# Layer 0's experts in a four-layer kernel: 64 own slots per expert instead of 128, two experts in one tile

## The chip, the cores and the metric

The kernel runs as one program on one core of a Trainium2 chip. A core has a matrix engine (TensorE; PE in the profile, PEld for the loading of its stationary operand), VectorE (DVE), ScalarE (ACT), GpSimd (POOL) and SyncE (SP). These work side by side and wait for each other through semaphores. 16 DMA engines move data between the device memory and the on-chip memory SBUF; matrix results land in the small on-chip memory PSUM. Transfers are put into queues by SP, by ACT and by POOL. All data is fp32.

The metric is the device time of one execution in microseconds (us). Before the change it is 2267.27 us, the median of three runs (2261.71 to 2273.08).

## What is computed

Tokens x of shape 2 x 512 x 256 (1024 tokens of width 256) go through four layers. Each adds a cross-attention to a context of 2 x 1024 x 256 and then a feed-forward part with eight experts. The change touches the feed-forward part of layer 0, in which each token goes to exactly one expert:

```python
def _L0_ffn_ref(hidden_states, router_w, router_b, w1, w2):
    x = hidden_states.reshape(-1, d)
    logits = x @ router_w + router_b
    route = softmax(logits, axis=1)
    max_prob = max(route, axis=1, keepdims=True)
    max_ind = argmax(route, axis=1)
    for e in range(num_experts):                 # 8
        h = x @ w1[e]                            # 256 -> 2 x 1024
        a, g = split(h, 2, axis=1)
        y = silu(a) * g @ w2[e]                  # 1024 -> 256
        out = where((max_ind == e)[:, None], y, out)
    return out * max_prob
...
x = x + _L0_ffn_ref(_layernorm(x, axis=-1), ...)
```

With the reference's inputs the router of layer 0 gives the eight experts 64, 19, 173, 147, 49, 28, 411 and 133 of the 1024 tokens.

## The kernel before

The kernel is written out in the order of the stages; a scheduling layer inserts the semaphore waits, and the order of instructions on each engine and of transfers in each queue is the order of the program, as the scheduler has laid it out. Names like `xs` or `w` are tiles; a pool gives each tag a fixed number of buffers (`bufs`), and a tile waits for the release of the buffer that it takes.

**Routing.** After layer 0's attention, `normed` gives the normalized tokens `xn`, `to_T` transposes them on TensorE into `xT`, and `router_logits` (L132, tile `pl`) forms the logits. `slots_of` (L332) ranks the tokens of each expert by a matmul with a triangular matrix (`pr`, L347 and L349) and gives each token a slot. An expert has 128 own slots, so slot tile e (128 rows of the array `xd`) belongs to expert e. What an expert has beyond 128 goes to overflow tiles of 128 rows, which are handed out in order of the experts. `wrow` holds, for each overflow tile, the rows of the weight array of its expert; `used` is the number of overflow tiles in use, read into a register. The thresholds, base numbers and triangular tables come as columns of one constant array, `c_route`.

**The tokens move.** `moe` scatters `xn` into `xd` by eight indirect transfers on POOL (L424, one for each 128 tokens). Then it calls a *filler* that gives TensorE something to do while this goes on: `first_batch` transposes the normalized context into `cT` and computes half of layer 1's keys and values in 16 jobs (`pk`, L555 and L575: a matmul group, a copy on ACT into one of two buffers, and a store to `kd` or `vd` through ACT's queue). The other half comes after the experts (`ahead1(..., 1)`).

**The slot tiles.** `slot_tile(s)` loads the weights of its expert, 128 partitions of 6144 numbers (3.1 MB), into `w`: the eight own tiles on SP's queue (L438), the overflow tiles by an indirect transfer on POOL's (L445). There are three `w` buffers. It reads its 128 rows of tokens (`xs`, L452), transposes them (`pt`, L460), copies them to `sT` (L462), and computes gate and up halves `pa` and `pg` (L132). Here 128 columns of weights are the stationary operand and the 128 tokens the moving one, so that the hidden activations come out transposed, as the next product needs them. ACT applies silu (L476), DVE multiplies (L477) into `hT`, the down product goes to `y` (L480), ACT copies it to `yo` (L507) and stores it to `yd`. Layer 0 always runs 8 own tiles and 6 overflow tiles (`ALWAYS`), in this order; a branch on `used > 6` (L501) runs a seventh. At the end `combine` gathers the rows of `yd` back to the tokens' order by eight indirect transfers on POOL (`yg`), multiplies by the gate and adds to X. Layers 1 to 3 use the same functions with their own sizes.

**What is next.** The attention of layer 1 reads `kd` and `vd` back: SP loads `kT` at L1021, and its first scores are at L1036.

Of the kernel before, what the change touches and what calls it, by code (L numbers as in the profile page):

```python
# [19 lines left out]
B = 2  # L20
# [13 lines left out]
def tile_kernel(ctx: ExitStack, tc: tile.TileContext, d: dict, out: bass.AP):  # L34
# [213 lines left out]
    def rt(name, shape=(TT, E)):  # L248
        return small.tile([P, *shape], F32, tag=f"rt_{name}", name=name, bufs=1)
# [81 lines left out]

    def slots_of(ps, picks, n_over):  # L332

        oh = rt("oh_all", (2 * TT + 1, E))
        nc.vector.memset(oh, 0.0)
# [8 lines left out]
        for k in range(1, TT + 1):  # L348
            nc.tensor.matmul(pr, ones, oh[:, TT - k : 2 * TT + 1 - k, :], start=False, stop=(k == TT))  # L349
        r = rt("rank_in", (TT + 1, E))  # L350
        nc.vector.tensor_copy(r, pr)
        more = rt("more", (E, 7))
        nc.vector.tensor_tensor(more, r[:, TT, :, None].to_broadcast([P, E, 7]), c_thr, ALU.is_gt)
        ov = rt("ov", (E,))
# [9 lines left out]
        nc.vector.scalar_tensor_tensor(  # L364
            sl, r[:, 0:TT, :], 128.0, base[:, None, :].to_broadcast([P, TT, E]), ALU.is_ge, ALU.mult
        )
# [35 lines left out]
    ALWAYS = {"L0": 6, "L1": 4, "L2": 11, "L3": 13}  # L402

    def moe(L, ps, hp, ep, rows, slots, wrow, used, F, act, glu, finish, filler=None, hold=None):

# [3 lines left out]

        n_over = wrow.shape[1]  # L410
        NS = E + n_over
        FT, W1 = F // P, (2 * F if glu else F)
# [21 lines left out]

        def slot_tile(s):
            w = ep.tile([P, WC], F32, tag="w", name="w")
            if s < E:
                x = nc.sync.dma_start(w, wd[s * P : (s + 1) * P, :]).ins  # L438
                if hold is not None and s < 4:
                    tc.add_manual_dep(  # L440
                        x, hold.name, mybir.DependencyInfo(mybir.DependencyClass.Sync, mybir.DependencyReason.DATA),
                        reason="not among the transfers that the attention waits for",
                    )
            else:
                nc.gpsimd.indirect_dma_start(  # L445
                    out=w, out_offset=None, in_=wd,
                    in_offset=bass.IndirectOffsetOnAxis(ap=wrow[:, s - E : s - E + 1], axis=0),
                )
            w1 = w[:, 0 : 2 * W1].rearrange("p (c f) -> p c f", c=2)
            w2 = w[:, 2 * W1 : 2 * W1 + FT * D].rearrange("p (t f) -> p t f", t=FT)  # L450
            xs = hp.tile([P, RW], F32, tag="xs", name="xs", bufs=4)
# [9 lines left out]
            sT = hp.tile([P, 2, P], F32, tag="sT", name="sT", bufs=3)  # L461
            nc.vector.tensor_copy(sT, pt)  # L462
            hT = hp.tile([P, FT, P], F32, tag="hT", name="hT")
            for f4 in range(0, FT, 4):
# [32 lines left out]

        always = E + ALWAYS[L]
        for s in range(always):
            slot_tile(s)  # L500
        with tc.If(used > ALWAYS[L]):  # L501
# [27 lines left out]

    def combine(hp, yd, slots, gates, dst):  # L530

        for t in range(TT):
            for i, si in enumerate(slots):
                yg = hp.tile([P, D], F32, tag="yg", name="yg", bufs=8)
                nc.gpsimd.indirect_dma_start(
                    out=yg, out_offset=None, in_=yd, in_offset=bass.IndirectOffsetOnAxis(ap=si[:, t : t + 1], axis=0)
                )
                to = dst[:, t, :]
                if gates is None:
                    nc.vector.tensor_add(to, to, yg)  # L540
                else:
                    nc.vector.scalar_tensor_tensor(to, yg, gates[i][:, t : t + 1], to, ALU.mult, ALU.add)
# [22 lines left out]
    def ahead1(ps, st, w, cT, b):  # L565

        if b == 0:
            kds["L1"] = dram.tile([B * 4 * P, S], F32, tag="L1kd", name="kd")
            vds["L1"] = dram.tile([B * S, 512], F32, tag="L1vd", name="vd")

        def values(pv, kt):
            r = slice(b * S + kt * P, b * S + (kt + 1) * P)
            mm2(pv, cT, r, w, slice(512, 1024))
            v = st.tile([P, 512], F32, tag="sv", name="sv", bufs=2)
            nc.scalar.copy(v, pv)  # L575
            nc.scalar.dma_start(vds["L1"][r, :], v)

        jobs = []
        for pr in range(4):
            for hf in range(2):  # L580
                jobs.append(("k", (b * 4 + pr) * P, hf * 512, slice(pr * P, (pr + 1) * P), b * S + hf * 512))
        jobs += [("v", kt) for kt in range(8)]
        ahead(ps, st, "L1", w, cT, jobs, values)
# [60 lines left out]
    def fill_slots():  # L644
# [6 lines left out]
        for L, NS, RW in (("L0", 15, D), ("L1", 15, D), ("L2", 23, D + 1), ("L3", 23, D + 1)):  # L651
            rows = NS * P + (2 * NT if RW > D else 0)
            xds[L] = [
                dram.tile([NS * P, RW], F32, tag=f"{L}xd", name="xd"), dram.tile([rows, D], F32, tag=f"{L}yd", name="yd")
            ]

            for to in xds[L][:1] if RW > D else (xds[L][0], xds[L][1][(E + ALWAYS[L]) * P :, :]):
                todo += [to[r : min(r + 4 * P, to.shape[0]), :] for r in range(0, to.shape[0], 4 * P)]
# [23 lines left out]
    with (  # L682
# [28 lines left out]
        route = load(const, [P, d["c_route"].shape[1]], d["c_route"], "route")  # L711
        c_thr = route[:, 0:56].rearrange("p (e j) -> p e j", e=E)
        c_tri = route[:, 56:120].rearrange("p (e f) -> p e f", e=E)
        c_iota = route[:, 120:240].rearrange("p (s e) -> p s e", e=E)
        c_base, c_first, c_part = route[:, 240:248], route[:, 248:256], route[:, 256:257]
        c_tok = route[:, 257:265]

# [223 lines left out]
    with (  # L941
        tc.tile_pool(name="L0f", bufs=1, reuse_waits="tile") as fp,
        tc.tile_pool(name="L0h", bufs=2, reuse_waits="tile") as hp,
        tc.tile_pool(name="L0g", bufs=3, reuse_waits="tile") as ep,
        psum(2, "L0fps") as ps,
    ):
        rw = load_rows(fp, d["L0_ffn_router_w"], "rw")
        rb = load_bc(fp, d["L0_ffn_router_b"], "rb")
        xT = fp.tile([P, 2, NT], F32, tag="xT", name="xT")
        xn = normed(fp, False)  # L950
# [9 lines left out]
        oh = first_of(lg, mp, "oh1")  # L960
        slots, wrow, used = slots_of(ps, [oh], 7)
        cT = fp.tile([P, 2, B * S], F32, tag="cT", name="cT")
# [6 lines left out]
        ahead1(ps, hp, wkv, cT, 1)  # L969
        combine(hp, yd, slots, [mp], X)  # L970

# [484 lines left out]
    with (  # L1456
# [28 lines left out]
        ahead16(ps, fp, "L2", params, 4)  # L1485
        combine(hp, yd, slots, None, X)

# [152 lines left out]
def _route():  # L1640


    e = np.arange(E, dtype=np.float32)
    row = np.concatenate([
        np.tile(128.0 * np.arange(1, 8), E),
        (e[None, :] < e[:, None]).ravel(),
        np.repeat(np.arange(15), E),
        128.0 * (E - 1 - e),
        128.0 * e,
    ]).astype(np.float32)  # L1650
    p = np.arange(P, dtype=np.float32)[:, None]
    return np.concatenate([np.tile(row, (P, 1)), p, p + 128.0 * np.arange(TT, dtype=np.float32)], axis=1)

# [105 lines left out]
```

## Time and profile before

| | us |
|---|---|
| median of three runs | 2267.27 |
| the profiled execution, its own time | 2271.06 |
| its span in the profile | 2269.0 |
| PE busy in it | 2087.4 |
| layer 0's slot tiles, first transpose to last product | 507.6 to 666.3 |
| the filler ahead of them | 471 to 508 |
| first scores of layer 1's attention | 706.98 |

The profile is one execution. Engines are busy side by side, so their busy times don't add up to the span. A row of the timeline gives start, duration, engine, line, operation, result and operands, shape and number of instructions; in brackets stands the idle time of the engine ahead of it and what ended it. A matmul in fp32 is recorded as several instructions: one logical matmul here is two records. The granted clock (PEclk) is the share of full speed at which TensorE may run; its mean over the execution is 0.962. DMA share is the mean share of time in which the 16 DMA engines are busy.

The weight transfers of layer 0's experts stand in the trace as follows:

| load | queue | issued at, us |
|---|---|---|
| own tiles 0 to 2 | SP | 459.75, 461.11, 469.9 |
| own tiles 3 to 7 | SP | 522.67, 533.3, 544.9, 555.5, 567.11 |
| overflow tiles 0 to 5 | POOL | 578.62, 589.58, 600.17, 611.79, 622.39, 634.01 |

The eight scatters into `xd` are at 492.52 to 502.6 on POOL, the reads `xs` begin at 504.62 on SP.

### The profile page before, as it was taken

The numbers are of one execution on the slowest core, as the hardware profiler recorded it, in microseconds if no ns is written. First come the engines' busy times: TensorE is split into PE (matmuls) and PEld (weight loads), VectorE is DVE, ScalarE is ACT, GpSimd is POOL, SyncE is SP. The second block draws the span as 40 slices with busy tenths as digits, with TensorE's granted clock in tenths as the row PEclk, the third lists the DMA queues.
The fourth block names the chain that finished last, engine by engine and source line by source line (L and its number), as shares of the span: only waits on it lengthen the run. The fifth ranks groups of instructions, "written<-read, shape, count | busy, mean of one in ns | idle before, by whom it ended". The sixth has DMA issues, their size and how long they took to land. (4 is left out here: it accounts for less than half of the span.)

```text
span 2269.0 us, 30730 instructions
## 1 busy us (share of the span) xinstructions
PE 2087.4 (92%) x11892; PEld 1267.6 (56%) x11892; DVE 1085.2 (48%) x2161; ACT 866.2 (38%) x1657; POOL 438.6 (19%) x420
## 2 busy tenths in 40 slices
PE   7999999999998999999898898899599999579996
PEld 3444444358984444555586344599333333479995
DVE  7766666741115656655313884110387773322223
ACT  4444444421115655555112333222135556223333
POOL 2222223210012111111101122312123310111110
PEclk9999999999999999999899999999789999689998
DMA  4222221277744101001454512687311101657771
GB/s 128 70 61 75 75 72 50 83 269 283 302 162 136 38 28 38 28 10 51 156 211 153 213 35 90 219 320 293 101 47 30 34 15 25 250 187 288 315 306 63
DMA packets 112328, 301.21 MB, mean 133 GB/s; under 512 B 23344, under 2 KB 76849, under 8 KB 103473
## 3 DMA queue, kind: packets, MB, share of 16 engines
q1 hardware_dynamic: 76624, 159.79, 21.0%
q0 software_dynamic: 9888, 104.49, 12.0%
q10 hardware_dynamic: 25664, 34.90, 4.3%
q8 instruction: 98, 1.61, 0.3%
q14 instruction: 54, 0.43, 0.1%
HBM read 243.42 MB, written 47.66 MB: 128 GB/s over the span
## 5 line engine op out<-in xcount | busy, mean ns | idle before, releaser
L1356 ACT ACTIVATE p<-s 128x512 f32<-128x512 f32 (+3 forms) x384 | 186.3, 546 | 176.2 <-PE s L1355 115.4
L132 PE MATMUL pa<-sT,w 128*128 128x128 f32 x1920 | 236.0, 277 | 10.7 <-DVE sT L462 3.7
L132 PEld LDWEIGHTS pa<-sT,w 128*128 128x128 f32 x1920 | 227.3, 193 | 19.3 <-ACT sq L1537 5.7
L480 PE MATMUL y<-w,hT 128*128 128x256 f32 x960 | 221.8, 383 | 12.4 <-DVE hT L477 6.3
L1298 PE MATMUL s<-kT,qT 32*128 32x512 f32 (+3 forms) x768 | 218.2, 613 | 10.0 <-DVE nm L1304 4.9
L480 PEld LDWEIGHTS y<-w,hT 128*128 128x128 f32 x960 | 178.5, 191 | 37.7 <-DVE hT L477 8.5
L1355 PE MATMUL s<-qA,kT 32*128 32x512 f32 (+3 forms) x768 | 196.1, 586 | 1.3 <-ACT p L1356 0.9
L1308 DVE TENSOR_REDUCE mx<-s 128x1 f32<-128x512 f32 x256 | 163.5, 686 | 56.1 <-PE s L1298 35.4
L477 DVE TENSOR_TENSOR hT<-act,pg 128x512 f32<-128x512 f32 x82 | 56.0, 688 | 233.5 <-PE pg L132 204.6
L1043 ACT ACTIVATE p<-s,nm 128x512 f32<-128x512 f32 x192 | 129.6, 687 | 84.0 <-DVE nm L1040 84.0
L132 PE MATMUL pg<-sT,w 128*128 128x128 f32 x1312 | 160.0, 275 | 1.3 <-ACT sv L575 1.3
L878 ACT ACTIVATE p<-s 128x1024 f32<-128x1024 f32 x128 | 124.3, 1023 | 89.7 <-PE s L873 89.7
L879 DVE TENSOR_SCALAR p<-p 128x1024 f32<-128x1024 f32 x128 | 108.9, 859 | 95.2 <-ACT p L878 95.2
L132 PEld LDWEIGHTS pg<-sT,w 128*128 128x128 f32 x1312 | 153.1, 192 | 1.4 <-ACT sv L575 1.4
L1040 DVE TENSOR_REDUCE nm<-s 128x2 f32<-128x1024 f32 x96 | 113.3, 1221 | 83.5 <-PE s L1036 83.5
L149 POOL TENSOR_TENSOR kT<-kT,turned 128x512 f32<-128x512 f32 x62 | 100.8, 1631 | 215.2 <-DVE turned L147 208.4
L884 DVE TENSOR_TENSOR acc<-acc,p 128x1024 f32<-128x1024 f32 x96 | 131.6, 1371 | 2.8
L804 PE MATMUL o<-p,v 128*64 128x512 f32 x512 | 125.7, 609 | 3.6 <-DVE p L879 3.6
L873 PE MATMUL s<-qT,kT 64*128 64x512 f32 x512 | 127.2, 615 | 0.0
L1298 PEld LDWEIGHTS s<-kT,qT 32*128 32x128 f32 x768 | 77.1, 191 | 66.7 <-issue 28.0
L1057 PEld LDWEIGHTS pt<-ident,p 128*128 128x128 f32 x768 | 86.3, 141 | 49.2 <-issue 24.5
L1331 PE MATMUL o<-p,v 128*32 128x256 f32 (+3 forms) x1280 | 106.2, 403 | 6.7 <-POOL p L1360 6.4
(282 smaller groups left out, 2955.3 us busy)
## 6 DMA issues: line engine op xcount, KB each, us to landing
w<-in_L_experts_dram SPq DMA_DIRECT2D x8, 3200.0 KB
w<-in_L_experts_dram SPq DMA_DIRECT2D x8, 3072.0 KB
w<-in_L_experts_dram SPq DMA_DIRECT2D x8, 2048.0 KB
w<-in_L_experts_dram SPq DMA_DIRECT2D x8, 1536.0 KB
kd<-sk ACTq DMA_DIRECT2D x40, 256.0 KB
kT<-kd SPq DMA_DIRECT2D x16, 512.0 KB
turned<-kT SPq DMA_DIRECT2D x60, 128.0 KB
v<-vd SPq DMA_DIRECT2D x12, 512.0 KB
```

What stands on the lines that cost most here:

```text
L132: nc.tensor.matmul(ps_ap, lhsT[:, dc, lcols], rhs[:, dc, rcols], start=(dc == 0), stop=(dc == 1))
L480: nc.tensor.matmul(y, hT[:, f, :], w2[:, f, :], start=(f == 0), stop=(f == FT - 1))
L804: nc.tensor.matmul(G[n]["o"][64 * j : 64 * j + 64, :], V[g, b][:, kt, pr * P + 64 * j : pr * P + 64 * j + 64], p[:, j, :], start=(kt == 0) ...
L873: nc.tensor.matmul(s1[:, j, :], G[n]["kT"][r, kt * P : (kt + 1) * P], G[n]["qT"][r, :], start=True, stop=True)
L878: G[n]["exp"] = nc.scalar.activation(p, s1, AF.Exp, scale=0.125).ins
L884: nc.vector.tensor_add(G[n]["acc"], G[n]["acc"], p)
L1040: nc.vector.tensor_reduce(nm[:, qt, :, c], s1, AX.X, ALU.max, negate=True)
L1043: nc.scalar.activation(p[:, j, :], s1[:, j, :], AF.Exp, bias=nm[:, qt, j, c : c + 1], accum_out=l[:, qt, j, c : c + 1],)
L1298: nc.tensor.matmul(s1[:, :w], qT[r, qt * P : (qt + 1) * P], kT[r, c * 512 : c * 512 + w], start=True, stop=True)
L1308: nc.vector.tensor_reduce(mx[:, qt, j, c : c + 1], s1, AX.X, ALU.max)
L1355: nc.tensor.matmul(s2[:, qs], kT[r, kt * P : (kt + 1) * P], qA[r, qs], start=True, stop=True)
L1356: nc.scalar.activation(p[:, j, qs], s2[:, qs], AF.Exp, scale=0.25)
```

## The change

In layer 0 each expert has 64 own slots. Two experts, 2s and 2s + 1, share *pair tile* s: its first 64 rows are slots of the one, the last 64 of the other. What an expert has beyond 64 tokens goes to overflow tiles of 128 rows, up to 11 of them. With the counts above 6 overflow tiles are in use, as before.

A pair tile loads both experts' weights on SP's queue. For gate and up the tokens are now the stationary operand, 64 columns at a time, and 512 columns of weights move. Tokens of the first expert write PSUM partitions 0 to 63, those of the second 64 to 127, in alternating matmuls. The hidden activations then stand with tokens on partitions, and are transposed on TensorE (`turn`) ahead of the down product, which works in the same two halves.

Order: pair 0, overflow 0, pair 1, overflow 1, pair 2, overflow 2, pair 3, overflow 3, overflow 4, overflow 5; the branch on `used > 6` holds five more. `FRONT` is the number of tiles of own slots.

Further edits: four `w` buffers in layer 0; its transposed tokens `xT` and `cT` share a buffer (tag "cT"); the values `sv` of the filler share the two buffers of `sk`; `combine` writes its gathers into one tile for all tokens (layer 0: in the buffer of `xn`) instead of eight rotating ones, for layers 0 and 1; the constant array is 80 columns wider. `yd`'s zero fill starts behind the ten tiles.

```diff
-    def slots_of(ps, picks, n_over):
+    def slots_of(ps, picks, n_over, first_of_expert=P):
+        c_thr, c_base, c_first = firsts[first_of_expert]
...
-        more = rt("more", (E, 7))
-        nc.vector.tensor_tensor(more, r[:, TT, :, None].to_broadcast([P, E, 7]), c_thr, ALU.is_gt)
+        nj = c_thr.shape[2]
+        more = rt(f"more{nj}", (E, nj))
+        nc.vector.tensor_tensor(more, r[:, TT, :, None].to_broadcast([P, E, nj]), c_thr, ALU.is_gt)
...
+    FRONT = {"L0": E // 2, "L1": E, "L2": E, "L3": E}
...
+        def pair_tile(s):
+            ws = []
+            for j in range(2):
+                w = ep.tile([P, WC], F32, tag="w", name="w")
+                nc.sync.dma_start(w, wd[(2 * s + j) * P : (2 * s + j + 1) * P, :])
+                ws.append(parts(w))
+            sT = turned_slots(s)[1]
+            hT = hp.tile([P, FT, P], F32, tag="hT", name="hT")
+            y = ps.tile([P, D], F32, tag="y", name="y")
+            hs = {}
+            def half(tag, c0):
+                pa = ps.tile([P, 512], F32, tag=tag, name="p" + tag)
+                for dc in range(2):
+                    for j in range(2):
+                        cols = slice(64 * j, 64 * j + 64)
+                        nc.tensor.matmul(
+                            pa[cols, :], sT[:, dc, cols], ws[j][0][:, dc, c0 : c0 + 512], start=(dc == 0), stop=(dc == 1)
+                        )
+                return pa
+            def hidden(c, pa, pg):
+                a = hp.tile([P, 512], F32, tag="act", name="act")
+                nc.scalar.activation(a, pa, act)
+                nc.vector.tensor_mul(a, a, pg)
+                hs[c] = a
+            def turn(c):
+                pt = ps.tile([P, 4, P], F32, tag="mm", name="pt")
+                for f in range(4):
+                    nc.tensor.transpose(pt[:, f, :], hs[c][:, f * P : (f + 1) * P], ident)
+                nc.vector.tensor_copy(hT[:, 4 * c : 4 * c + 4, :], pt)
+            def product(c):
+                for f in range(4 * c, 4 * c + 4):
+                    for j in range(2):
+                        cols = slice(64 * j, 64 * j + 64)
+                        nc.tensor.matmul(
+                            y[cols, :], hT[:, f, cols], ws[j][1][:, f, :], start=(f == 0), stop=(f == FT - 1)
+                        )
+            pa = half("a", 0)
+            hidden(0, pa, half("g", F))
+            pa = half("a", 512)
+            turn(0)
+            hidden(1, pa, half("g", F + 512))
+            product(0)
+            turn(1)
+            product(1)
...
-        for s in range(always):
-            slot_tile(s)
+        if front == E:
+            for s in range(always):
+                slot_tile(s)
+        else:
+            for s in range(front):
+                pair_tile(s)
+                slot_tile(front + s)
+            for s in range(2 * front, always):
+                slot_tile(s)
...
-                yg = hp.tile([P, D], F32, tag="yg", name="yg", bufs=8)
+                yg = rows[:, t, :]
...
-            v = st.tile([P, 512], F32, tag="sv", name="sv", bufs=2)
+            v = st.tile([P, 512], F32, tag="sk", name="sv", bufs=2)
...
-        tc.tile_pool(name="L0g", bufs=3, reuse_waits="tile") as ep,
+        tc.tile_pool(name="L0g", bufs=4, reuse_waits="tile") as ep,
...
-        xT = fp.tile([P, 2, NT], F32, tag="xT", name="xT")
+        xT = fp.tile([P, 2, B * S], F32, tag="cT", name="xT")
...
-        slots, wrow, used = slots_of(ps, [oh], 7)
+        slots, wrow, used = slots_of(ps, [oh], 11, 64)
```

## The prediction

> **What bounds the kernel now.** I read the busy totals first, then the stage that the change touches in windows, then single instructions in it.
>
> ```profile
> PE 2087.4 (92%) x11892; PEld 1267.6 (56%) x11892; DVE 1085.2 (48%) x2161; ACT 866.2 (38%) x1657; POOL 438.6 (19%) x420
> ```
>
> ```profile
> 475.00:480.00 5.00, 5.00 (x36) 3.92 (x35) 1.07 (x2) 1.82 (x4) 0.00 (x0) 1.00 1.01 429
> 507.60:666.30 158.70, 153.95 (x1150) 145.66 (x1148) 24.47 (x42) 23.54 (x44) 5.69 (x6) 1.00 0.67 257
> 710.00:715.00 5.00, 3.87 (x12) 1.55 (x13) 2.35 (x3) 3.65 (x12) 0.71 (x1) 0.71 1.12 264
> ```
>
> The columns after the window and its length are busy PE, PEld, DVE, ACT, POOL, then granted clock, DMA share and GB/s. From 507.6 to 666.3 layer 0's 14 slot tiles run: PE is busy for 153.95 of 158.70 us, the DMA engines for 0.67. So this stage is bound by TensorE, at 158.7 / 14 = 11.3 us a tile. One tile in the timeline of PE:
>
> ```profile
> 566.91 1.95 PE L132 MATMUL pa<-sT,w 128*128 128x128 f32 x16
> 568.70 1.95 PE L132 MATMUL pg<-sT,w 128*128 128x128 f32 x16
> 570.49 1.95 PE L132 MATMUL pa<-sT,w 128*128 128x128 f32 x16
> 572.27 1.95 PE L132 MATMUL pg<-sT,w 128*128 128x128 f32 x16
> 574.06 3.62 PE L480 MATMUL y<-w,hT 128*128 128x256 f32 x16
> 577.51 0.60 PE L460 MATMUL pt<-ident,xs 128*128 128x128 f32 x4
> ```
>
> From start to start: four groups of 1.79 us, one of 3.45, transposes 0.57, and the rest up to 11.3 is the wait for the copy sT. A tile of 3.1 MB of weights arrives in less time than that: the SP load issued at 567.11 runs its packets from 568.0 to 576.2, 9.1 us from issue to landing, and the one that POOL issues at 634.01 ends at 643.5, after 9.5.
>
> **What is removed and added.** The router's counts, from the reference's inputs, are 64, 19, 173, 147, 49, 28, 411 and 133 tokens per expert. Beyond 128 own slots that is 45, 19, 283 and 5 tokens, 1 + 1 + 3 + 1 = 6 overflow tiles of 128, as the trace has (six indirect loads). Beyond 64 it is 109, 83, 347 and 69, and again 1 + 1 + 3 + 1 = 6. So 14 tiles become 4 pair tiles and 6 slot tiles, the branch of further tiles stays skipped, and the 14 weight loads stay 14.
>
> **A pair tile.** Its gate and up halves are 4 logical matmuls each, stationary 64 columns, moving 512. The nearest row has that shape and puts two heads into the two column halves:
>
> ```profile
> 426.31 1.94 PE L804 MATMUL o<-p,v 128*64 128x512 f32 x8
> 428.17 3.72 PE L861 MATMUL po<-wo,oT 128*128 128x256 f32 x16
> ```
>
> Eight records, which are 4 logical matmuls, take 1.86 us to the next start, 0.232 a record, where the full-width form pk 128*128 128x512 takes 0.43 to 0.45. So the halves do run together. Four groups: 7.44. Transposes of hidden activations: 16 records at 0.13 (103.0 us for the 768 of pt<-ident,p): 1.9 with their turn. The product: 16 logical, 32 records, moving 256; the po row above has 0.232 a record unpaired, halved 0.116: 3.72. With pt 0.57, the copy sT 0.65 and about 0.5 of waiting for silu (0.60) and product (0.69) that the next half doesn't hide, a pair is 14.8 us, against 22.6 for two tiles. If the column halves did not overlap, it would be 4 x 1.72 + 3.72 = 10.6 more. DVE has 3.2 us in a pair (0.42 + 4 x 0.69), ACT 1.6 (2 x 0.60 + 0.37), both hidden. Stage on PE: 4 x 14.8 + 6 x 11.2 = 126.4, so **-32.3** (bounds: -34, halves overlapping and nothing waited for; +10, not at all).
>
> The Trainium skill's "TensorE: Matmul & The Clock Gate", section "Measured speedup vs the span model", gives three column tiles 2.38 times one, which is 0.79 of ideal. Two at that efficiency would make a half 3.58/1.59 = 2.25 us, and by this estimate the four pairs would be 10 us dearer; the L804 row has 1.86 and no sign of it.
>
> **Weights inside the stage.** A pair needs two buffers at once and frees two at once. There are now four buffers. The loads rotate w0, w1, o0, w2, then w3 in w0's buffer and o1 in w1's, so at the end of a pair SP's load for the next pair and POOL's load for the tile behind it start together, and only one slot tile of 11.2 us lies between. One load alone already has the DMA engines at share 1.01 (window 475:480), so the two need 2 x 8.2 = 16.4 us of transfer. If SP's went first it would land 9.1 us after release and nothing would wait; if they share, both land at about 17.2 (0.9 to begin, 16.4). No row of before has two weight loads side by side. The nearest row is a store beside a load:
>
> ```profile
> 474.43 0.34 ACTq L559 DMA_DIRECT2D kd<-sk  x1
> ...
> 486.28 0.59 ACT L555 COPY sk<-pk 128x512 f32<-128x512 f32 x1 [1.30 <-DMA kd<-sk]
> ...
> 499.69 0.59 ACT L575 COPY sv<-pk 128x512 f32<-128x512 f32 x1 [1.16 <-DMA vd<-sv]
> ```
>
> A 256 KB store that is issued at 474.43, under the weight loads, holds its buffer till 486.28; near 499.69, without them, a buffer comes round every 1.7 us. So the queues share the engines in turn, and I take sharing: 17.2 - 11.2 - 1.0 (the pair's own pt and sT fit into the wait) = 5.0, three times: **+15** (bounds 0 and 17.4).
>
> The skill's "DMA: Bandwidth & Descriptors", section "Queues, rings and completion order", says that each engine goes round the queues packet by packet. By it both loads land near 17, as in the sum; first come first served would give 0 here and a sum 15 us lower.
>
> **The clock.** At 706.98 and 710.91 PE idled 2.09 and 1.95 us, and window 710:715 has a granted clock of 0.71: half speed for one stretch of 3.4 us, 1.7 us lost. Each of the three waits of 5 us should do the same: **+5.1** (bounds 0, and 10 with two such stretches each).
>
> **The front of the stage.** Before, two loads start on SP at 459.75 and 461.11, while attention still runs, and the third at 469.9. In the changed program's order three wait for the last out-projection, 468.3, so 3 x 3.15 MB at 0.43 MB/us end at 492 instead of 485. Then POOL's o0 gather, which the order puts ahead of the eight xd scatters (0.96 us each, every 1.27) and behind the indices wrow (ready near 490.6), runs 8.2 us more; behind the scatters queue xs on SP, and behind cTr (2 MB, 4.9 us), now ahead of xs, too. The filler (16 jobs of 1.72 us on PE, 471 to 508 before, L1's keys and values from pk) lies under all of it, and each job's store goes out under weight packets: 8 packets of each engine, one for each weight packet of 0.91 us, some 8 us a store, with two buffers. xT and cT share a buffer, so the filler also starts only after the router's logits (481.8 before, about 477.4 now, with most C transposes behind them). By about 504 some 4 stores are out and 6 jobs done; 10 x 1.72 from there is 521. PE has nothing else, since the first pair's transposes stand behind all 16 jobs. So the stage starts near 520.5 instead of 507.6: **+12.5** (bounds +3.7, the filler never held: logits 477.4, copies, 27.5 of jobs, 2.2 of ranking, some 4 of C transposes, 511.7; and +16, the stores held till xs lands). The scatters end near 502 and hide under the filler; with a filler unheld they would be next.
>
> **Behind the stage.** L1's first kT load (697.31) waited for stores that now end sooner, and PE waited 2.09 us for it: **-1.5** (bounds -2, 0). The eight yg gathers go to a tile of their own, hidden as before. The ranking has 64 instead of 56 thresholds per row, one more zero store and a longer skipped branch: under 0.5 us together, **0**; without the filler over them they would be seen.
>
> **Sum.** -32.3 + 15 + 5.1 + 12.5 - 1.5 = -1.2 against the profiled execution's 2271.06 us (span 2269.0, 2.1 around it): 2269.9. That execution lies 3.8 above the median 2267.27, so I predict 2266 on the median's scale: the TensorE time that the packing frees is given back to DMA.
>
> **Rivals.**
> *Faster: the loads don't collide.* If SP's load lands first, or the filler's stores aren't held, the sum is -1.2 - 20.1 = -21 (no waits, so no half clock), or -1.2 - 8.8 = -10. For it: on average there is room (ten loads of 3.15 MB within some 130 us are 242 GB/s, of about 430). Against it: the kd row above. The two times are 2246 and 2257, 2237 with both; I put 2246. Chance 0.36.
> *Slower: the waits cool the clock for longer and the front is held.* With the clock at half for two stretches after each wait (+5) and the front at +16 (+3.5) the sum is +7; with waits of 5.8, +10; with any loss of pairing in the column halves, of which a quarter is 10 us, +20: 2287. It decides once such terms reach +12.5 in all. Chance 0.23. For it: half-clock stretches in the trace do run longer after a big wait. Against it: L804.
> *The change doesn't do what it says.* The halves run one after the other: +42, 2308. Against it the same row; 0.02. A seventh overflow tile by rounding of the router would run five more tiles, 57 us: 0.01: expert 0 has exactly 64, one more would need a tile.
>
> **How the numbers follow.** Within 0.5% (11.3 us, about what a measurement of this kernel can tell from no change) is my forecast, 0.38. Faster is 0.36, since either of two large terms, loads and front, need only fall out; slower is 0.23 + 0.02 + 0.01 = 0.26, since it needs several bounds at once. The range takes in the faster rival, down to 2243, and the slower to 2286; the forecast's own is 2257 to 2278.
>
> **What would show it.** Right: groups pa and pg of the pairs at 0.23 us a record; the first pair's transposes near 520; PE idle of 5 us ahead of the second, third and fourth pair, released by DMA into w, with a clock under 1.0 after each; the stage's end near 665. Wrong: records at 0.45 (pairing), a start near 512 (stores not held), waits under 1 us (loads in turn), or any of the later layers moving by more than 2 us, for which I have no term.

## The result, and the profile after

The changed kernel takes 2269.23 us in the median of 12 runs (2262.59 to 2275.51), the kernel before, in the same series, 2266.86 us (2261.71 to 2273.65). The ratio is 1.0006, with a 95% interval from 0.999 to 1.0022. Nothing that can be measured has changed in the whole, though 21 us have gone from the stage that was changed. The profiled execution has a span of 2269.7 us (2269.0 before) and a mean clock of 0.958 (0.962).

First the busy line of the page of the kernel after: TensorE has 23.6 us less work than before.

```profile
PE 2063.8 (91%) x11532; PEld 1208.1 (53%) x11532; DVE 1083.0 (48%) x2157; ACT 859.2 (38%) x1645; POOL 439.3 (19%) x420
```

The stage itself, in windows of the kernel after (busy PE, PEld, DVE, ACT, POOL, then clock, DMA share, GB/s):

```profile
500.00:505.00 5.00, 0.00 (x0) 0.00 (x0) 0.00 (x0) 0.00 (x0) 2.13 (x3) 0.84 0.91 319
529.10:666.20 137.10, 122.69 (x789) 85.57 (x787) 23.07 (x38) 18.29 (x33) 4.74 (x5) 0.96 0.62 252
```

From the first pair's transposes to the last product it takes 137.1 us in place of 158.7. But it starts at 529.15, where before it started at 508.0: both end at 666. And ahead of it there is a window in which TensorE does nothing at all, while the DMA engines are busy for 0.91 of the time.

Where the time went, from instants that both timelines have:

| stretch | before, us | after, us | difference | predicted |
|---|---|---|---|---|
| to the first slot transposes | 508.00 | 529.15 | +21.2 | +12.5 |
| from there to the last product's end | 158.3 | 137.05 | -21.3 | -12.2 |
| from there to layer 1's first scores (706.98, 712.68) | 40.7 | 46.5 | +5.8 | -1.5 |
| from there to the end of the span | 1562.0 | 1557.0 | -5.0 | 0 |
| sum | | | +0.7 | -1.2 |

The last line needs care: nothing of the change lies in that stretch. In the twelve traces of the experiments below, which share its code, 1555.6 to 1563.3 us pass from the first scores to the end. So 5 us either way there is what two executions differ by, and a single profile's end doesn't tell the effect of an edit of that size.

*A pair tile and the wait for its weights.* The second pair in the timeline of PE, kernel after:

```profile
551.02 3.62 PE L547 MATMUL y<-w,hT 128*128 128x256 f32 x16
554.47 0.38 PE L454 MATMUL pt<-ident,xs 128*128 128x128 f32 x2
555.42 1.04 PE L477 MATMUL pa<-w,sT 128*64 128x512 f32 x2 [0.56 <-ACT yo L581]
559.79 2.82 PE L477 MATMUL pa<-w,sT 128*64 128x512 f32 x5 [3.33 <-DMA w<-in_L_experts_dram]
```

and the two weight loads that the end of the first pair releases, in the timelines of SP's and POOL's queues:

```profile
543.86 11.14 SPq L465 DMA_DIRECT2D w<-in_L_experts_dram  x2
...
544.15 0.98 POOL L524 DMA_INDIRECT w<-in_L_experts_dram,wrow  x1 [36.20 <-PE y L498]
```

They are issued 0.3 us apart (a row with x2 stands for two issues; the second of the SP row is the load after that). By the packets in the trace, SP's load has the engines to itself at first: POOL's moves its first packet at 549.1, 5.0 us after its issue (4.4 and 4.3 us at the next two pairs), and from there on the two share. The pair begins on the half whose weights are there (two records at 555.42), then waits until 559.79: 15.9 us after the issue. The next two pairs wait 2.65 and 2.78 us, 15.3 and 15.4 after the issue. After the first of these waits the clock is down:

```profile
555.00:560.00 5.00, 1.26 (x4) 0.41 (x6) 0.32 (x1) 0.04 (x1) 0.00 (x0) 0.81 0.94 403
560.00:565.00 5.00, 5.00 (x14) 1.34 (x14) 0.00 (x0) 0.60 (x1) 0.00 (x0) 0.51 1.01 431
```

The first pair, which waits for nothing, takes 14.6 us (529.15 to 543.77). The others take 20.6, 17.4 and 19.3, so waits and half clock together cost 6.0 + 2.8 + 4.7 = 13.5 us.

*The front.* ACT's copies of the filler's results, kernel after:

```profile
494.81 0.58 ACT L629 COPY sk<-pk 128x512 f32<-128x512 f32 x1 [4.67 <-DMA kd<-sk]
...
507.54 0.58 ACT L629 COPY sk<-pk 128x512 f32<-128x512 f32 x1 [11.10 <-DMA kd<-sk]
...
516.41 0.58 ACT L629 COPY sk<-pk 128x512 f32<-128x512 f32 x1 [6.68 <-DMA kd<-sk]
```

In brackets is the time that ACT stood idle before the copy and what ended it: a store to kd had to land before its buffer was free. The first long wait lies under the overflow load that POOL issued at 492.59, the second under cTr, which SP issued at 507.52.

Two more things made the front late. TensorE's clock was lowered during the waits, so that the last 24 records of the filler, from 517.05, take 12.1 us, some 1.8 more than 24 of the 32 that took 13.7 us before:

```profile
515.00:520.00 5.00, 2.95 (x4) 1.40 (x5) 0.00 (x0) 1.17 (x2) 0.00 (x0) 0.71 0.55 211
```

And the first tokens `xs` are read only at 520.62, where before it was 504.62; a filler that ended earlier would soon have met that.

*Behind the stage.* DVE in the kernel after, at the start of layer 1:

```profile
685.56 0.17 DVE L82 TENSOR_TENSOR rsq<-rsq,r 128x8 f32<-128x8 f32 x1
698.68 3.28 DVE L98 TENSOR_SCALAR xn<-X,mv,rsq 128x256 f32<-128x256 f32 x8 [12.96 <-PE pk L132]
```

The normalized tokens of layer 1 were ready to be written at 685.7 and waited 12.96 us for the filler's last matmul. Before, the same instruction ran at 688.23. The skipped branch shows as well: the second half of the filler starts 1.74 us behind the last product, where before it was 0.82 (kernel before, then after):

```profile
667.38 14.00 PE L132 MATMUL pk<-cT,wkv 128*128 128x512 f32 x32 [0.82 <-ACTq L501]
668.01 13.97 PE L132 MATMUL pk<-cT,wkv 128*128 128x512 f32 x32 [1.74 <-ACTq L575]
```

### The profile page after: what moved, and what is told of

The parts are those of the page before. It is cut to its first block, busy times and chain, and to the rows that moved or that the text cites. A ratio compares the mean times of both kernels' runs of the same rounds, so it can differ in the third digit from the quotient of the medians.

```text
span 2269.7 us, 29982 instructions
## 1 busy us (share of the span) xinstructions
PE 2063.8 (91%) x11532; PEld 1208.1 (53%) x11532; DVE 1083.0 (48%) x2157; ACT 859.2 (38%) x1645; POOL 439.3 (19%) x420
## 3 DMA queue, kind: packets, MB, share of 16 engines
q8 instruction: 97, 1.59, 0.3%
## 5 line engine op out<-in xcount | busy, mean ns | idle before, releaser
L132 PE MATMUL pa<-sT,w 128*128 128x128 f32 x1664 | 205.0, 278 | 8.7 <-DVE sT L456 3.7
L132 PEld LDWEIGHTS pa<-sT,w 128*128 128x128 f32 x1664 | 197.1, 193 | 17.2 <-ACT sq L1613 5.8
L547 PE MATMUL y<-w,hT 128*128 128x256 f32 x832 | 192.8, 384 | 9.3 <-ACT hT L537 4.3
L547 PEld LDWEIGHTS y<-w,hT 128*128 128x128 f32 x832 | 154.7, 192 | 31.7 <-DVE hT L544 6.1
L132 PE MATMUL pg<-sT,w 128*128 128x128 f32 x1056 | 129.3, 276 | 0.0
L544 DVE TENSOR_TENSOR hT<-act,pg 128x512 f32<-128x512 f32 x66 | 45.0, 687 | 169.7 <-PE pg L132 147.9
L132 PEld LDWEIGHTS pg<-sT,w 128*128 128x128 f32 x1056 | 123.9, 193 | 0.0
L148 POOL TENSOR_TENSOR kT<-kT,cos 128x512 f32<-128x512 f32 x62 | 87.8, 1425 | 134.7 <-DMA turned<-kT 63.4
```

What stands on the lines that cost most here:

```text
L132: nc.tensor.matmul(ps_ap, lhsT[:, dc, lcols], rhs[:, dc, rcols], start=(dc == 0), stop=(dc == 1))
L547: nc.tensor.matmul(y, hT[:, f, :], w2[:, f, :], start=(f == 0), stop=(f == FT - 1))
```

## The experiments

All are edits of the changed kernel and compute the same. Ratios are to the kernel before, run beside them on the same chip; the chip is not the same for all experiments.

### Loads one after the other

```diff
+                if front < s < 2 * front < E + 1:
+                    tc.add_manual_dep(x, last["w"].name, ...)   # POOL's load waits for SP's
```

> The overflow load that follows a pair's end (POOL) now starts only when SP's load for the next pair has landed; nothing else changes. Theory (two loads released together share the DMA engines and both land at about 16 us): SP's load lands about 9.3 us after the pair's end, before the slot tile between is over, so the three waits of 3.33, 2.65 and 2.78 us and the half clock after them go. The stage from the first pair's transposes to the last product falls from 137.1 to about 124 us, the whole by about 13 us, ratio to before near 0.995. Rival (the loads come late because they are issued late or because one load alone takes that long): the waits stay, the stage stays at 137.

2263.79 us, ratio 0.9969 (0.9952 to 0.9986). The three waits are gone, and the stage falls from 137.1 to 129.0 us. One wait has come in their place, in the timeline of PE of this run:

```profile
571.15 3.75 PE L132 MATMUL pa<-sT,w 128*128 128x128 f32 x16 [4.86 <-DMA w<-in_L_experts_dram,wrow]
```

It is a slot tile that waits now, for the overflow load of 554.04, which shares the engines with SP's next load of 553.26. So sharing is confirmed and the rival falls; 8 of the 13 us come back.

```diff
+                if s > 1 and j == 0:
+                    tc.add_manual_dep(last["w"], last["o"].name, ...)   # and SP's next for POOL's
```

> As in the run turns, and SP's next load after that waits in its turn for the overflow tile's load. Theory: in the run turns the wait of 4.86 us that came in place of the three was the overflow load sharing with the next SP load; in turn, each load lands some 9.3 us after the one before and no wait of more than 2 us is left in the stage, which falls from 137.1 to 124 to 127 us. Rival (strictly one after the other, ten loads with a gap of 1 us at each are themselves the bound): waits of 3 us and more turn up at the later pairs and the stage stays at 129 or above.

2267.78 us, ratio 0.9981 (0.9956 to 1.0006); the stage takes 134.7 us. The wait of the slot tile is gone, waits of 1.73 and 2.91 us at the third and fourth pair are back. The rival had it: strictly one after the other, the loads themselves come too late. The run is inconclusive in its time, not in its trace.

### The first overflow load later

```diff
+                if s == front < E:
+                    tc.add_manual_dep(x, last["xs"].name, ...)   # behind the first xs
```

> The first overflow tile's load starts only when the first slots have been read (and the third expert's load, which the order places behind it, with it), so 6.3 MB of weights leave the time in which the filler stores its results. Theory (the filler is held by its stores, which go out one packet for each weight packet): the filler ends some 13 to 16 us earlier, the first pair's transposes move from 529.2 to about 514, and the whole falls by as much if the load is landed when the pair ends. Rival (the filler is late because it starts after the logits, since xT and cT share a buffer): the start moves by 3 us at most.

2268.18 us, ratio 1.0001 (0.9983 to 1.0019): nothing gained. But the trace shows the filler's time move as expected, and what then stops the pair:

```profile
496.67 13.90 PE L132 MATMUL pk<-wkv,cT 128*128 128x512 f32 x32
510.40 0.38 PE L457 MATMUL pt<-ident,xs 128*128 128x128 f32 x2
523.95 3.68 PE L480 MATMUL pa<-w,sT 128*64 128x512 f32 x8 [13.17 <-ACT sv L662]
```

The last eight jobs run without a gap (13.90 us, as before the change), the first transposes come at 510.4 in place of 529.15. Then the first pair's matmul waits 13.17 us for a copy of the filler: its PSUM tile `pa` is the one that a job's `pk` had, and this copy waits for a store that lies under the two loads which now start at 504.4 and 505.7:

```profile
504.84 0.33 ACTq L663 DMA_DIRECT2D vd<-sv  x1
523.32 0.58 ACT L662 COPY sv<-pk 128x512 f32<-128x512 f32 x1 [17.23 <-DMA vd<-sv]
```

The cause is borne out, but the wait only moved: from the filler to the pair behind it. The 18.8 us are not the overflow load's alone. The attention ends 2.1 us earlier in this trace (its last projection is at 463.88 in place of 466.00), and cTr is issued at 482.69 in place of 507.52, which the edit does not name. That cTr matters less is suggested by the run serial_long below, in which cTr came at 498.43, beside the overflow load, and the first transposes at 527.4 all the same.

```diff
+            for e, k in ((1, 1), (2, 3), (0, 0)):                      # the first three loads, on SP
+                nc.sync.dma_start(ts[k], wd[e * P : (e + 1) * P, :])
...
+                    tc.add_manual_dep(x, stored["L1"].name, ...)       # first overflow load behind the last vd store
```

> The loads for experts 1 and 2 come first on SP, into the two buffers that lie over nothing the attention still needs, expert 0's third; the first overflow tile's load waits for the last store of the filler. So the weights are in by about 484, and no weight packet runs beside the filler's stores after that. Theory (filler held by stores beside weights, and the first pair held by the last of these stores): the filler ends near 511, the first pair's first matmul comes at 512 to 514 and not at 530.1 or, as with the load only somewhat later, at 524 behind a starved store; the whole falls by some 15 us. Rival (the whole front is bound by the late start of the filler): first matmul after 520.

2265.86 us, ratio 0.9977 (0.9954 to 1.0000). The overflow load now waits for the filler's last store. First transposes at 515.85 and the first pair's matmul at 516.80, so the rival falls, but the expected 512 to 514 and the 15 us in all were missed: the next matmuls have waits of 1.49 and 2.10 us, and 1.40 for the overflow load, which had become a little late. The part meant to be early was not: the three SP loads still started near 468, because the pool gave the first of them the buffer that lies over a tile of the attention's last projection (the next run moves the buffers, and its loads start early).

> Only the four weight buffers of layer 0 are placed otherwise (and yo has two buffers in place of three, to make room): the loads for experts 1 and 0 go into memory that the attention has left by about 460, expert 2's comes third at 468, in the manner of the kernel before; in front_early and all_three the three loads still began at 468, since the first of them lay over a tile of the last projection. The first overflow load stays ahead of the scatters. Theory (each 3.1 MB of weights that runs beside the filler costs it about 7 us of stores): with some 9 us less of weights beside it, the filler ends 6 to 9 us earlier, the first pair's transposes at 517 to 521 in place of 525 to 529. Rival (what holds the filler is the overflow load and cTr alone): 524 or later.

```diff
-        tc.tile_pool(name="L0g", bufs=4, reuse_waits="tile") as ep,
+        tc.tile_pool(name="L0g0", bufs=1, ...) as e0, ... as e1, ... as e2, ... as e3,
+        ep = Ring([e3, e1, e0, e2])        # w0, w1, o0, w2
```

2263.36 us, ratio 0.9975 (0.9961 to 0.9990). The first loads are back before the end of the attention, as in the kernel before; the first transposes come at 523.3. In the seven traces whose front is as in the change (its own, turns, turns2, l1_place, l1_free, serial, serial_long) they come at 525.2 to 529.2. That is 2 to 6 us earlier, short of the 6 to 9 that were expected and close to the rival's 524. A part of the gain is lost ahead of the front: the attention's last projection comes at 468.83, where it is at 463.6 to 467.3 in the seven, and counted from it the transposes come 5.5 to 8.7 us earlier. cTr moved here too (490.76), so how much is due to the loads that start late is not separated. o0_late, which moved the overflow load, had 510.4.

### The start of layer 1

```diff
-        xT = cp.tile([P, 2, NT], F32, tag="xT", name="xT")
-        to_T(ps, xT, normed(cp, True, "oT"), TT, g_l, b_l, "s")
+        xn = normed(cp, True, "oT")
+        xT = cp.tile([P, 2, NT], F32, tag="xT", name="xT")
+        to_T(ps, xT, xn, TT, g_l, b_l, "s")
```

> Only places in SBUF change: in layer 0 xn is laid below xT and cT, in layer 1 xn below xT, so that layer 1's xn no longer lies over cT. Theory (layer 1's normalized tokens wait for the filler's last matmul, 12.96 us of idle DVE before them, because they lie over cT): that wait goes, and from the last product of layer 0 (666.2) to the first scores of layer 1 (712.7) it is about 41 us in place of 46.5; the whole falls by about 5. Rival (the filler's results sharing two buffers holds it, or the kT fetch is late by itself): 46 us stay.

2270.94 us, ratio 1.0010 (0.9989 to 1.0032). The tokens no longer wait, and it gains nothing: 46.3 us from the stage's end to the first scores. In its place there is a longer wait for the keys:

```profile
702.62 1.88 PE L132 MATMUL pq<-xT,wq 128*128 128x512 f32 x4
709.33 3.78 PE L1113 MATMUL s<-kT,qT 64*128 64x512 f32 x8 [4.83 <-POOL kT L149]
```

The kT load was issued at 698.87, 0.8 us after the issue of the filler's last store had ended; kT lies over buffers that these stores are sent from.

> As in l1_place, and the two buffers of the filler's results lie in a place of their own, under no tile of layer 1's first fetch. Theory (in l1_place the first kT fetch waited for the last store, since kT lay over the buffers it is sent from): the fetch is issued some 5 us or more before the filler's end, and from the last product of layer 0 to the first scores it is 41 to 43 us in place of 46.3. Rival (the fetch waits for something else, the gathers or all stores to kd): still 45 or more.

```diff
+        tc.tile_pool(name="L0s", bufs=2, reuse_waits="tile") as skp,
-        ahead1(ps, hp, wkv, cT, 1)
+        ahead1(ps, skp, wkv, cT, 1)
```

2269.51 us, ratio 0.9996 (0.9971 to 1.0021): the time shows nothing. The kT load is issued at 694.70, ahead of the last store, and from the stage's end to the first scores it is 43.5 us, just above what was expected. This stretch varies from one execution to the next: 44.6 to 47.1 us in the eight traces of the changed kernel and its edits that have neither of these two edits, 42.7 to 45.0 in the four that have both. By the means, 46.2 and 43.7, the two overlaps in memory cost some 2.5 of the 5.8 us. Of the rest, 0.8 is the skipped branch (1.64 us here, 0.82 before), and the transposes of `xn` have a wait of 2.58 us for `sv`, where before it was 0.24; the wait of 1.59 for `sk` has its like before (1.85). That these are the whole rest was not tried.

### Column halves in another order

```diff
-                for dc in range(2):
-                    for j in range(2):
+                for j in range(2):
+                    for dc in range(2):
...
-                for f in range(4 * c, 4 * c + 4):
-                    for j in range(2):
+                for j in range(2):
+                    for f in range(4 * c, 4 * c + 4):
```

> In a pair tile the matmuls of the first expert's column half all come before those of the second, within each half and each product; the same matmuls, another order. Theory (two column halves run at once when their matmuls alternate): the overlap goes, a half takes about 3.5 us in place of 1.75 and a product group of 16 records 3.7 in place of 1.85, so a pair grows by about 10 us, the stage by 40 less what the waits for weights give back (13): whole +27 to +40, ratio 1.012 to 1.018. Rival (the matmuls are fast for another reason, such as a moving operand of 512 columns): nothing changes.

2267.82 us, ratio 0.9994 (0.9975 to 1.0014). A clear miss: gate and up lose nothing, the product loses half of what was expected. The first pair of this run:

```profile
526.20 1.94 PE L477 MATMUL pa<-w,sT 128*64 128x512 f32 x8 [0.56 <-ACT sv L649]
527.94 1.94 PE L477 MATMUL pg<-w,sT 128*64 128x512 f32 x8
...
533.88 2.81 PE L498 MATMUL y<-w,hT 128*64 128x256 f32 x16
```

Halves of four and four records still take 1.74 us, runs of eight and eight 2.74 to the next start in place of 1.83. That is 12 record times of 0.23, not 8 and not 16: as if one half may run some four records ahead of the other in program order.

```diff
-                for f in range(4 * c, 4 * c + 4):
-                    for j in range(2):
+                for j in range(2):
+                    for f in range(FT) if c else ():
```

> The down product of a pair is put behind both groups of transposes and goes through the first expert's 8 logical matmuls before the second's. In the run serial, 8 records of one half and then 8 of the other took 2.81 us where alternating ones take 1.88, and 4 and 4 of gate and up lost nothing. If a half can run ahead of the other by 4 records, the group of 12 and 16 records takes (12 + 16 - 4) x 0.232 = 5.6 us; if the halves did not overlap at all 6.5; if order did not matter 3.7.

A single run, 2261.57 us. Its product, and the loads that follow it:

```profile
538.77 5.45 PE L498 MATMUL y<-w,hT 128*64 128x256 f32 x28
...
541.60 0.33 SPq L465 DMA_DIRECT2D w<-in_L_experts_dram  x1
...
544.49 0.98 POOL L524 DMA_INDIRECT w<-in_L_experts_dram,wrow  x1 [31.24 <-PE y L498]
```

5.38 us to the next start, near the 5.6 of the theory; the halves do overlap, and the order matters once runs are longer than about four records. The other thing it shows was not looked for: the first expert's weights are read to the end earlier, so SP's load starts 2.9 us ahead of POOL's, and no pair waits for weights any more. The stage takes 130.1 us though its products are slower. Two things come together there, the earlier start and the shorter sharing (the last packet of SP's load ends 12.6 us after its issue, in place of 14.5), and no run separates them. In the run serial the head start was 1.2 us, and waits of 0.70 and 0.26 were left.

### All together

The edits of front_early, turns2 and l1_free in one kernel, and no others.

> front_early, turns2 and l1_free together. If the three places are where the saving of the pair tiles went, they add up: first pair at 512 (-17), stage at 124 to 127 (-11), layer 1's start (-4), some 30 us in all: median about 2238, ratio to before 0.985 to 0.990. If the time is held elsewhere (later layers give back what comes earlier), the ratio stays above 0.995.

2261.38 us, ratio 0.9956 (0.9934 to 0.9978). Less than the sum. The stage takes 142.7 us: the first pair waits 4.37 us for a copy of the filler, whose last stores lie beside cTr (issued at 508.83), and turns2's waits are there again. The loads started at 468.05, as in front_early. The ratio is the rival's, its reason is not: from the first scores to the end it takes 1555.6 us, so the later layers give nothing back.

```diff
-    cTr = load_rows(crp, d["ctxT"], "cTr")
+    x = nc.sync.dma_start(cTr, ...).ins
+    tc.add_manual_dep(x, stored["w"].name, ...)     # behind the fourth overflow load
```

with the edits of early_loads, turns and l1_free, and the first overflow load behind the last vd store.

> early_loads, the first overflow load behind the filler's last store, turns (not turns2: its stage was 129.0 against 134.7), l1_free, and cTr (2 MB, first read in layer 2) behind the loads of the stage. Theory: the first pair at 509 to 513, its first matmul within 3 us of it, the stage at 127 to 130, layer 1's first scores some 43 us after it: 682 to 686 in place of 712.7, the whole about 2240, ratio 0.985 to 0.990. Rival (a further wait takes the place of those removed, as in all_three): ratio 0.993 or more.

2250.15 us, ratio 0.9923 (0.9901 to 0.9944). First pair at 516.1, stage 133.8 us with two waits of slot tiles (5.29 and 4.68), 42.7 us to layer 1's first scores at 692.7. The front and the stage are slower than expected, and the ratio lies between the theory's and the rival's. Both waits are for overflow loads, as the one in turns.

In the last kernel the edit of turns is taken out of best, and that of serial_long put in.

> As best, but without the overflow loads waiting for SP's (turns); in its place the product order of serial_long, by which the first expert's weights are read to the end some 2.9 us before the second's. In serial_long SP's load began 2.9 us ahead of POOL's and no wait for weights was left, in place of 3.33, 2.65 and 2.78 us. Theory (two loads share the engines, and a head start of 2.9 us is enough for the one that is needed first): no wait of over 1 us in the stage, which takes about 130 us as in serial_long against 133.8 in best, and the whole some 4 us less than best: ratio about 0.990. Rival (in serial_long the waits went because its front was later): waits of 3 us at the later tiles, ratio 0.992 or more.

2246.66 us, ratio 0.9913 (0.9899 to 0.9927). The stage in the timeline of PE (third pair and the tile after it):

```profile
563.27 3.62 PE L588 MATMUL y<-w,hT 128*128 128x256 f32 x16
574.48 1.03 PE L525 MATMUL y<-w,hT 128*64 128x256 f32 x4
576.10 5.45 PE L525 MATMUL y<-w,hT 128*64 128x256 f32 x28
581.48 0.66 PE L465 MATMUL pt<-ident,xs 128*128 128x128 f32 x4
582.48 2.02 PE L132 MATMUL pa<-sT,w 128*128 128x128 f32 x16 [0.35 <-issue]
```

No wait for weights is left; the stage runs from 512.9 to 642.0, 129.1 us, and the first scores come at 686.9 in place of 712.7. This is the fastest version, 19 us below the kernel before. Its interval and that of best overlap (0.9899 to 0.9927 and 0.9901 to 0.9944), and the ratios are of different chips; that its stage is shorter is shown by one trace of each, that it is faster than best is not shown by the times.

## Why the prediction was right, step by step

The forecast of no change, and its reason, held: the packing frees TensorE, and the loads and the front take it back. That the sum came out within 2 us is luck: against their terms the stage is 9.1 us better and the rest of the execution 5.0, while the front is 8.7 us worse and the start of layer 1 7.3. The 5.0 are within what two executions differ by, so the 2 us by which the prediction would have called a move of the later layers a sign of being wrong were too narrow.

- *The pair tile, 14.8 us and -32.3 for the stage on PE.* Right in kind: 14.6 for the first pair; the stage without its waits is 137.1 - 13.5 = 123.6 against 126.4, as a slot tile behind a pair takes 10.7 and not 11.2. Inside the pair errors cancel: the halves take 6.9 us in place of 7.44 (1.74 each and not 1.86), and the hidden activations are turned in 8 records and not 16, 1.1 us in place of 1.9; but the transposes of the tokens, the copies and the waits take 2.9 in place of 1.72. The estimate against it, from the figure for three column tiles in the Trainium skill ("TensorE: Matmul & The Clock Gate", "Measured speedup vs the span model"), 0.79 of ideal, doesn't hold here: two halves at once take 1.74 where two one after the other would, by estimate, take 3.44 (8 records of 0.43).
- *Loads in pairs share the engines, +15.* Right in mechanism, shown by turns, and serial_long and stagger agree; the size was 8.8 (3.33 + 2.65 + 2.78). The pairs went on 15.3 to 15.9 us after the issue of SP's load, not 17.2, as the two loads do not start together: POOL's moved its first packet 4.3 to 5.0 us after its issue. And part of each wait lay under the pair's own transposes and first matmuls, which need only the half that is there. While both run, the trace has packets of both queues side by side, as the Trainium skill's "DMA: Bandwidth & Descriptors", "Queues, rings and completion order", states (the engines go round the queues packet by packet); one load alone had taken 9.1.
- *The clock, +5.1.* 4.7 measured (13.5 - 8.8), in a different spread: much after the first and third wait, next to nothing after the second.
- *The front, +12.5.* The mechanism was right, the term was mis-sized by 8.7 us. I had the stores freed "by about 504". The trace has them held until 507.5 by the overflow load, and then, a step that I counted only in SP's order and not against the stores, until 516.4 by cTr. Some 1.8 us of it are the lowered clock in the filler, which the clock's term counted for the pairs alone. The scatters, which the step had done near 502, were late too: the eighth was issued at 506.97.
- *Behind the stage, -1.5.* Wrong, with the sign: +5.8. The step said that the first kT load "waited for stores that now end sooner". I had followed the semaphores of one transfer and not the memory: the new layout puts layer 1's xn over cT and kT over the filler's buffers, so both wait for the end of the filler. l1_free gave back some 2.5 of it.
- *The edits costed at 0.* The gathers' own tile and the ranking's wider tables show no wait that was not there before. The skipped branch does: 0.9 us more (1.74 in place of 0.82), where less than 0.5 was allowed for all of these together. The shared `sk` buffers, which I didn't cost, show waits of 1.4 and 1.0 us in the second half of the filler, where before there was one of 1.85.

Of the rivals, *faster* named the two terms that held the time, and the last run took both away by hand: with the loads staggered and the front free, and l1_free's edits and the later cTr besides, the kernel is 19 us faster, where -30 was worked out for loads and front. *Slower* had a front of +16, and it was worse still (+21.2); with layer 1's start that is more than the +12.5 by which it was to decide. It did not come because the waits took 8.8 us and not 15 to 17, and the stage's own work was 2.8 us less than predicted. That the change doesn't do what it says fell with the first row of a pair.

## What to carry to other kernels

When a tile frees two big buffers at once and two queues refill them, the transfers share the engines, and the one that is needed first is held up by the other: give it a head start of a few us, by the order in which the buffers are read to the end, rather than forbid the second transfer to run. Before moving big loads, look for small stores that run beside them and for who waits for their buffers, up to the PSUM tile that the next stage takes. And after any change of a pool's size, compare which later tiles lie over which earlier ones; two of the waits here came from addresses alone.

## What the runs showed of the hardware

Matmuls on the two 64-column halves of the array overlap even when they don't alternate: runs of four records lose nothing, runs of eight take 2.74 us in place of 1.83, a run of 12 and 16 takes 5.38. The filler's copies, each of which needs the buffer of an earlier 256 KB store, follow each other every 1.7 us in free flow, which is the time of a job on TensorE; beside one stream of weight loads a copy waited 11.1 us, beside two 17.2. A weight load on POOL's queue moved its first packet 1.7 to 2.3 us after its issue in the kernel before, with no other load beside it, and 4.3 to 5.5 us after it in the kernel after, beside a load on SP's queue. After waits of 3.33 and 2.78 us the granted clock was lowered, to 0.51 and 0.71 in a window of 5 us; after one of 2.65 us it stayed at 1.00.
